# The experts' leftover rows: five blocks of 128 rows replaced by two groups of four blocks of 32 rows

## The chip, the cores and the metric

The kernel runs on one core of one Trainium2 chip. The time is that of the device in microseconds (us). A core has TensorE (PE, matrix products; its weight loads are listed as PEld), VectorE (DVE), ScalarE (ACT), GpSimd (POOL) and SyncE (SP), which run their own instruction streams in order and wait for one another through semaphores, and 16 DMA engines which all queues share.

## The reference

Two layers over x of 2 x 2048 tokens with 256 features, all in float32. Layer 0 adds gated linear attention and a product with quantised weights. Layer 1 adds softmax attention with 16 heads and, for every token, two of eight experts:

```python
logits = xf @ gate_W.T
pi = _sinkhorn(-logits)
_, top_idx = jax.lax.top_k(pi, TOP_K)
g = jnp.einsum('nd,efd->enf', xf, W_gate)
u = jnp.einsum('nd,efd->enf', xf, W_up)
y = jnp.einsum('enf,edf->end', jax.nn.silu(g) * u, W_down)
for k in range(TOP_K):
    out = out + y[top_idx[:, k], n_ar] * pi[:, k:k + 1]
```

D is 256 and F is 1024. As each of 4096 tokens goes to two experts, there are 8192 rows of expert work. With the reference's own inputs the eight experts get 1047, 977, 950, 1003, 1054, 1044, 1029 and 1088 rows.

## The kernel before

Layer 0 runs over strips of 512 tokens and leaves the sum x + layer 0 in `acc`, 128 partitions by 32 tiles of 128 tokens by 256 features (32 KB in each partition). Layer 1's attention adds to `acc` in 2 x 512-token pieces through the "chores" of `normalise`, and as soon as a 512-token piece is complete, SP writes it from `acc` to the output in memory (L1816). After that the piece of `acc` isn't used again. Attention is written as units: `scores` (L1824, tiles of 32 rows by 128 columns), the exponential on ScalarE (L1830) and `weighted_sums` (L1846), in which TensorE works in four column tiles of 128 rows by 32 columns: each tile has its own 32 stationary columns and its own moving operand, and writes its own 32 partitions of PSUM. A weighted sum comes two units after its scores.

Beside attention, VectorE runs the `router` in small steps, one for each unit: Sinkhorn, the two best experts of each token, and then `Routing.steps`, which gives each (token, expert) pair a row in a table in memory. An expert with `count` rows gets `(count + 127) >> 8` full blocks of 256 rows, and what is left over, up to 128 rows, goes to one half block of 128 rows. Room in the table that no pair takes points to a spare row of the output. `sends` fetches normed rows and scatters them into the table from POOL (L2139), each scatter behind the one before. `over` sets the flag `more` when there are more than 32 full or more than 5 half blocks; only then a branch after the usual way works through the rest.

Then come the experts: `Experts.pieces` goes through the blocks, 32 full ones with a half one after 8, 14, 20, 26 and 32 of them. For block n:

- POOL gathers its expert's weights, gate and up together 2 MB, down 1 MB (L2169), two blocks ahead; SP loads its rows (`xb`, L2185).
- `open_rows`: TensorE transposes the rows (L2207), ScalarE copies them (L2211), VectorE picks each row's routing weight and destination.
- `hidden`: for each of 8 chunks of 128 hidden features, four matmuls (L2229) with the weights stationary and the rows moving (256 columns, or 128 in a half block), then SiLU on ScalarE (L2234) and the product with up on VectorE (L2235).
- `add_rows`, one block later: 8 matmuls for each 128 rows (L2245), VectorE scales (L2250), and POOL adds the rows to the output by an indirect DMA with addition (L2254). These DMAs all write the output, so each is issued after the one before has landed.

On TensorE the order is: hidden of n, transposes of n+1, second product of n-1, hidden of n+1. A scheduler orders the instructions of each engine from the program and its data; instructions given to `keep_in_program_order` keep theirs. `rooms` hands out storage: gate and up weights go to attention's operands `operands.heads`, down weights partly there and partly to the tiles of `pt`, and all h_ps, x_ps and attention's PSUM tiles share seven banks.

Of the kernel before, what the change touches and what calls it, by code (L numbers as in the profile page):

```python
# [86 lines left out]
NHALF = NE  # L88
NBLK = NFULL + NHALF
ROWS = NFULL * BS + NHALF * BS // 2  # L90
FULLS, HALVES = 2 * B * N // BS, 5
# [132 lines left out]
def two_layers(ctx: ExitStack, tc: tile.TileContext, a: dict, out: bass.AP):  # L224
# [20 lines left out]
    )  # L245
    c.mine = const.tile([P, NBLK, NE], F32, tag="mine", name="mine")
    c.wrow = const.tile([P, NBLK], I32, tag="wrow", name="wrow")
    c.half_bias = const.tile([P, E], F32, tag="half_bias", name="half_bias")
# [10 lines left out]
    blocks = list(range(FULLS))  # L259
    for i in range(HALVES):  # L260
        blocks.insert(FULLS - 6 * i, NFULL + i)
    usual_way(tc, a, out, c, blocks)
# [4 lines left out]
    with where(c.special):  # L267
        with where(c.more):
            layer1_experts(tc, a, out, c, [b for b in range(NBLK) if b not in blocks])
        with where(c.general):  # L270
            general_way(tc, a, out, c)
# [3 lines left out]
def usual_way(ctx, tc, a, out, c, blocks):  # L275
# [27 lines left out]
    attention(tc, a, out, acc, la, norms, spans, c, operands, ready, routing, blocks, vector)  # L303
# [3 lines left out]
def general_way(ctx, tc, a, out, c):  # L307
# [17 lines left out]
    layer1_experts(tc, a, out, c, range(NBLK))  # L325
# [1359 lines left out]
def attention(  # L1685
    ctx, tc, a, out, acc, la, norms, spans, c, operands, ready, routing, blocks, vector
# [194 lines left out]
    def rooms(name, n, shape, dt=F32):  # L1881

        if name == "wgateup":
            return operands.heads[(0, 1, 3)[n % 3]].rearrange("p j t -> p (j t)")
# [25 lines left out]
    experts = Experts(tc, a, out, c, rooms, blocks)  # L1910
# [37 lines left out]
class Routing:  # L1948
# [28 lines left out]
    def steps(self, pool, psum, pi):  # L1977
# [76 lines left out]
        full, half = blocks[:, 0, :], blocks[:, 1, :]  # L2054
# [3 lines left out]
        vector.tensor_tensor(half, count, in_full, ALU.is_gt)  # L2058
        yield
        end = blocks  # L2060
        for step in (1, 2, 4):
# [12 lines left out]
        vector.tensor_tensor(away, end[:, 1, :], half, ALU.subtract)  # L2074
        vector.scalar_tensor_tensor(away, end[:, 0, :], -2.0, away, ALU.mult, ALU.add)
        vector.tensor_scalar(
            away, away, float(BS // 2), float(NFULL * BS), ALU.mult, ALU.add
# [23 lines left out]
        for n, bs in enumerate((slice(0, NFULL), slice(NFULL, NBLK))):  # L2101
# [10 lines left out]
            self.c.mine, self.eidx.unsqueeze(1).to_broadcast([P, NBLK, NE]),  # L2112
            expert.unsqueeze(2).to_broadcast([P, NBLK, NE]), ALU.is_equal,
        )
        row = tile_("row", [P, NBLK])
        vector.tensor_scalar(row, expert, float(P), self.pidx, ALU.mult, ALU.add)
        vector.tensor_copy(self.c.wrow, row)
        over = self.over
        for n, done in enumerate((FULLS, HALVES)):
# [36 lines left out]
class Block:  # L2156


    def __init__(self, e, n, b):
        self.e, self.n, self.b = e, n, b  # L2160
        self.tiles = NC if b < NFULL else NC // 2
        self.rows = self.tiles * P
        self.first = b * BS if b < NFULL else NFULL * BS + (b - NFULL) * BS // 2
# [95 lines left out]

class Experts:  # L2260


    def __init__(self, tc, a, out, c, rooms, blocks):
        self.tc, self.nc, self.a, self.out, self.c = tc, tc.nc, a, out, c
        self.rooms = rooms
        self.todo = [Block(self, n, b) for n, b in enumerate(blocks)]

    def pieces(self, begun=False):
# [4 lines left out]
        todo = self.todo  # L2273
        if not begun:
# [3 lines left out]
        for n, block in enumerate(todo):  # L2278
# [9 lines left out]
            if n and not last:  # L2288
                todo[n - 1].add_rows()
            yield  # L2290
        todo[-1].add_rows()


@with_exitstack
def layer1_experts(ctx, tc, a, out, c, blocks):
    p2 = ctx.enter_context(tc.tile_pool(name="moe", bufs=2))
    psum = ctx.enter_context(tc.tile_pool(name="moeps", bufs=2, space=PSUM))
    bufs = {"wgateup": 3, "wdown": 4, "xb": 4, "y": 4, "by": 4, "wt": 4, "to": 4,
            "h_ps": 4}

    def rooms(name, n, shape, dt=F32):
        pool = psum if name.endswith("_ps") else p2
        return pool.tile(shape, dt, tag=name, name=name, bufs=bufs.get(name, 2))

    for _ in Experts(tc, a, out, c, rooms, blocks).pieces():
        pass
# [165 lines left out]
```

## Time and profile before

| | us |
|---|---|
| median of 3 runs | 1641.2 (1638.37 to 1641.56) |
| the profiled execution | 1644.31 |
| its span, first to last instruction | 1642.5 |
| mean granted TensorE clock | 0.988 of full speed |
| L2229, hidden, 256 columns | 2048 records, 447.8 busy |
| L2229, hidden, 128 columns | 320 records, 36.7 busy |
| L2245, second product | 1104 records, 245.0 busy |
| experts, from the first L2229 to the last L2245 | 895.99 to 1630.2 |

A float32 matmul is two records, one for each of two passes, and each has its own weight load. [...]

### The profile page before, as it was taken

How to read it: one execution, taken by the hardware profiler on the slowest of the kernel's cores; microseconds unless marked ns; L12 is line 12 of the kernel's file. 1: busy time of each engine (PE TensorE's matmuls, PEld its weight loads, DVE VectorE, ACT ScalarE, POOL GpSimd, SP SyncE). 2: the span in 40 equal slices, each digit the busy share in tenths (PEclk: the TensorE clock that was granted, in tenths of full speed). 3: DMA queues.
4: the chain of work that ended last, by engine and by line, in shares of the span. 5: the costliest groups of instructions: out<-in, count | busy, mean ns of one | idle time of the engine just before them, and what ended most of it. 6: DMA issues, size and time to landing. Idle time of an engine off the chain costs nothing.

```text
span 1642.5 us, 33089 instructions
## 1 busy us (share of the span) xinstructions
PE 1587.1 (97%) x13786; PEld 1300.2 (79%) x13786; DVE 719.9 (44%) x2224; ACT 751.5 (46%) x1469; POOL 389.7 (24%) x350
## 2 busy tenths in 40 slices
PE   7789999999999999999999999999999999999997
PEld 4557676667688887888877888888898898888886
DVE  6787676564478766344353222222222222222221
ACT  5354555553688888998987211121111111111110
POOL 4342221221200003233321122222222232222221
PEclk9899999999899999999999999999999999999998
DMA  9710112213530402611144555555565565556531
GB/s 260 195 39 28 54 54 64 71 53 73 156 49 8 78 16 79 137 62 62 61 157 162 192 178 177 180 180 177 180 198 198 164 219 197 167 168 202 177 90 19
DMA packets 82510, 204.41 MB, mean 124 GB/s; under 512 B 8624, under 2 KB 64304, under 8 KB 71728
## 3 DMA queue, kind: packets, MB, share of 16 engines
q0 software_dynamic: 24944, 138.33, 26.0%
q1 hardware_dynamic: 56304, 62.71, 14.3%
q8 instruction: 110, 1.80, 0.5%
q10 hardware_dynamic: 1104, 1.18, 0.2%
q14 instruction: 48, 0.39, 0.1%
HBM read 152.26 MB, written 49.92 MB: 123 GB/s over the span
## 4 chain that ended last, share of the span: by engine, by line
PE 89%; DVE 7%; POOL 2%; DMA 1%; issue 1%; ACT 1%; POOLq 0%; SPq 0%; DVEq 0%; ACTq 0%
PE h_ps L2229 29%; PE y_ps L2245 14%; PE sc L1824 12%; PE o_ps L1846 10%; PE vf_ps L540 3%; PE y_ps L540 3%; PE f_ps L1808 2%; PE tr L590 2%; PE vg_ps L540 2%; PE g_ps L540 2%; PE qk_ps L540 1%; PE q_ps L540 1%; PE o_tr L1781 1%; PE o_ds_ps L540 1%; PE x_ps L2207 1%; PE k_ps L540 1%
## 5 line engine op out<-in xcount | busy, mean ns | idle before, releaser
L2229 PE MATMUL h_ps<-va,qk 128*128 128x256 f32 (+1 forms) x2368 | 484.5, 365 | 0.0
L2229 PEld LDWEIGHTS h_ps<-va,qk 128*128 128x128 f32 x2368 | 425.6, 190 | 53.6 <-issue 0.3
L1830 ACT ACTIVATE pt<-sc,shift 128x512 f32<-128x512 f32 (+3 forms) x687 | 405.2, 702 | 55.2 <-ACT pt L1830 26.7
L2234 ACT ACTIVATE sg<-h_ps 128x256 f32<-128x256 f32 (+1 forms) x296 | 109.4, 370 | 600.2 <-PE h_ps L2229 590.8
L2235 DVE TENSOR_TENSOR larger<-sg,h_ps 128x256 f32<-128x256 f32 (+1 forms) x296 | 119.4, 404 | 358.4 <-ACT sg L2234 346.1
L1824 PE MATMUL sc<-qk 32*128 32x128 f32 (+6 forms) x3916 | 226.0, 337 | 2.0 <-PE norm_ps L540 1.1
L1824 PEld LDWEIGHTS sc<-qk 32*128 32x128 f32 x3916 | 185.9, 187 | 37.4 <-ACT pt L1830 15.6
L1846 PE MATMUL o_ps<-pt,va 128*32 128x128 f32 (+6 forms) x3916 | 189.2, 320 | 3.1 <-DVE o_sb L114 3.1
L1846 PEld LDWEIGHTS o_ps<-pt,va 128*32 128x32 f32 x3916 | 141.2, 110 | 34.3 <-issue 9.3
L2254 POOL DMA_INDIRECT out<-va,to x69 | 109.9, 1593 | 210.9 <-DMA out<-va,to 76.2
L114 DVE TENSOR_TENSOR pt<-pt,keepmask 128x128 f32<-128x128 f32 (+3 forms) x546 | 120.0, 278 | 73.7 <-ACT pt L1830 71.9
L2245 PE MATMUL y_ps<-qk,larger 128*128 128x256 f32 x560 | 124.6, 379 | 0.1
L2250 DVE SCALAR_TENSOR_TENSOR va<-y_ps,wt,half_bias 128x256 f32<-128x256 f32 x69 | 30.4, 480 | 208.2 <-PE y_ps L2245 208.2
L2245 PE MATMUL y_ps<-larger 128*128 128x256 f32 x544 | 120.4, 379 | 0.0
L2245 PEld LDWEIGHTS y_ps<-qk,larger 128*128 128x128 f32 x560 | 104.7, 190 | 13.8 <-DVE larger L2235 0.5
L2245 PEld LDWEIGHTS y_ps<-larger 128*128 128x128 f32 x544 | 102.0, 190 | 13.1
L2139 POOL DMA_INDIRECT table<-rows,place x64 | 64.7, 1011 | 182.0 <-DMA table<-rows,place 145.2
L2169 POOL DMA_INDIRECT qk<-in_wgateup,wrow x37 | 36.8, 994 | 188.9 <-PE h_ps L2229 161.0
L540 PE MATMUL vf_ps<-qk,xnT 128*128 128x512 f32 x128 | 58.0, 606 | 0.0
L114 DVE COPY o_sb<-o_ps 128x256 f32<-128x256 f32 x64 | 27.0, 423 | 47.6 <-PE o_ps L1846 44.0
L2169 POOL DMA_INDIRECT qk<-in_wdown,wrow x19 | 18.4, 970 | 120.8 <-PE y_ps L2245 83.6
L540 PEld LDWEIGHTS vf_ps<-qk,xnT 128*128 128x128 f32 x128 | 24.0, 193 | 28.8 <-issue 25.2
(252 smaller groups left out, 1708.1 us busy)
## 6 DMA issues: line engine op xcount, KB each, us to landing
xb<-table SPq DMA_DIRECT2D x32, 265.0 KB
qk<-qk SPq DMA_DIRECT2D x32, 256.0 KB
qk<-qk SPq DMA_DIRECT2D x64, 128.0 KB
table<-spare SPq DMA_DIRECT2D x3, 2120.0 KB
va<-v SPq DMA_DIRECT2D x4, 1208.0 KB
v<-v SPq DMA_DIRECT2D x8, 574.0 KB
normed<-xn SPq DMA_DIRECT2D x8, 512.0 KB
rows<-normed POOLq DMA_DIRECT2D x16, 256.0 KB
```

Source lines behind the costliest of these rows:

```text
L114: return lambda *a, **k: self.tc.keep_in_program_order(begin(*a, **k))
L540: tc.keep_in_program_order(nc.tensor.matmul(*args, **kwargs))
L1824: nc.tensor.matmul(scs[r][:, at : at + q1 - q0], lhsT=heads[rows, 1, kb * P : (kb + 1) * P], rhs=heads[rows, 0, qt * QT + q0 : qt * QT + q ...
L1830: nc.scalar.activation(pt[:, r, 0:width], scs[r][:, 0:width], AF.Exp, bias=shift)
L1846: nc.tensor.matmul(o_ps[r * HR : (r + 1) * HR, to + q0 : to + q1], lhsT=values[b, way][:, kb, h * VC : h * VC + HR], rhs=pt[:, r, at : at ...
L2139: self.nc.gpsimd.indirect_dma_start(out=self.c.table, in_=rows[:, n, :], in_offset=None, out_offset=bass.IndirectOffsetOnAxis(ap=to[:, 2 * ...
L2169: e.nc.gpsimd.indirect_dma_start(out=w, out_offset=None, in_=e.a[name], in_offset=bass.IndirectOffsetOnAxis(ap=e.c.wrow[:, self.b : self.b ...
L2229: nc.tensor.matmul(ps[:, j, rows], lhsT=self.wgu[:, j, c, f * P : (f + 1) * P], rhs=self.xT[:, c, rows], start=c == 0, stop=c == 1,)
L2234: nc.scalar.activation(sg, ps[:, 0, rows], AF.Silu)
L2235: nc.vector.tensor_tensor(self.hT[:, f, rows], sg, ps[:, 1, rows], ALU.mult)
L2245: nc.tensor.matmul(ps[:, c, :], lhsT=self.hT[:, fc, c * P : (c + 1) * P], rhs=self.wd[:, fc, :], start=fc == 0, stop=fc == NFC - 1,)
L2254: nc.gpsimd.indirect_dma_start(out=out, out_offset=bass.IndirectOffsetOnAxis(ap=self.to[:, c : c + 1], axis=0), in_=y[:, c, :], in_offset= ...
```

## The change

The half blocks go. What an expert has left over, still up to 128 rows, goes into blocks of 32 rows, as many as it needs. Four such blocks, of whatever experts, make a `Group` of 128 table rows. The usual way works through 32 full blocks and two groups (8 small blocks); the flag `more` is set when there are more.

In a group the parts are swapped: the rows are stationary (32 columns for each block, in TensorE's four column tiles) and the weights move, 512 columns at a time for gate and up and 256 for down. The hidden values come out by row, so they are transposed in eight steps before the second product. The weights of the four blocks' experts come in three parts of 4 x 1 MB (gate, up, down), one after another, in the room of `acc`, a quarter for each block; each part is fetched when the products with the one before are issued. The steps of the groups stand at ends of full blocks: for group 0 the load after block 3, the opening after 6, gate after 7, up after 11, the transposes after 12, down after 15; for group 1 the same after 16, 19, 20, 24, 25 and 28. A group's result goes out in four scatters, one for each block, in which the rows of the other three blocks go to spare rows.

Routing counts the small blocks, has 67 block entries where it had 43, and makes `nowhere` (spare rows) and `wpart` (the rows of the half-width weights) besides. The size of the table stays as it was. The branch for `more` works through full blocks and groups in two passes; its code and that of the general way are left out here.

```diff
+SB = 32
+NSMALL = 4 * NE
+NBLK = NFULL + NSMALL
+ROWS = NFULL * BS + NSMALL * SB
+FULLS, GROUPS = 2 * B * N // BS, 2
...
-    blocks = list(range(FULLS))
-    for i in range(HALVES):
-        blocks.insert(FULLS - 6 * i, NFULL + i)
-    usual_way(tc, a, out, c, blocks)
+    usual_way(tc, a, out, c)
...
+        if name == "group_w":
+            return acc.rearrange("p t e -> p (t e)").rearrange("p (r f) -> p r f", r=4)
+        if name in ("group_b", "group_x", "group_h", "group_y"):
+            tag = {"group_b": "on", "group_x": "on", "group_h": "o_sb", "group_y": "onT"}[name]
+            return p2.tile(
+                [P, ST], F32, tag=tag, name=name, bufs=1 if tag == "onT" else 2
+            )[:, 0 : shape[1]]
+        if name == "group_s":
+            return p2.tile(shape, F32, tag="sk_equal", name=name, bufs=1)
...
-        vector.tensor_tensor(half, count, in_full, ALU.is_gt)
+        vector.tensor_tensor(small, count, in_full, ALU.is_gt)
+        for n in range(1, BS // 2 // SB):
+            one = tile_(f"small{n}", [P, NE])
+            vector.scalar_tensor_tensor(one, in_full, float(n * SB), count, ALU.add, ALU.is_lt)
+            vector.tensor_tensor(small, small, one, ALU.add)
...
+        for r in range(4):
+            rows = slice(r * SB, (r + 1) * SB)
+            vector.tensor_tensor(
+                self.c.mine[rows, NFULL:, :],
+                self.eidx[rows, :].unsqueeze(1).to_broadcast([SB, groups, NE]),
+                by_group[rows, :, r : r + 1].to_broadcast([SB, groups, NE]), ALU.is_equal,
+            )
+        yield
...
+        nowhere = tile_("nowhere_f", [P, 4])
+        vector.tensor_scalar(
+            nowhere, self.pidx.to_broadcast([P, 4]), float(SPARE), None, ALU.add
+        )
+        vector.tensor_copy(self.c.nowhere, nowhere)
+
+        for n in range(2):
+            part = tile_(f"part{n}", [P, NSMALL])
+            vector.tensor_scalar(
+                part, row[:, NFULL:], 2.0, float(n), ALU.mult, ALU.add
+            )
+            vector.tensor_copy(self.c.wpart[:, n, :], part)
...
+class Group:
+    def __init__(self, e, g):
+        self.e, self.g = e, g
+        self.b = NFULL + 4 * g
+        self.first = NFULL * BS + g * P
+        self.tiles = [slice(r * SB, (r + 1) * SB) for r in range(4)]
+
+    def gather(self, name, part):
+        e = self.e
+        rows, first = (e.c.wpart[:, part, :], NFULL) if name == "wgateup" else (e.c.wrow, 0)
+        self.w = e.rooms("group_w", 0, [P, 4, 2 * FF])
+        for r in range(4):
+            e.nc.gpsimd.indirect_dma_start(
+                out=self.w[:, r, :], out_offset=None,
+                in_=e.a[name].rearrange("r (j f) -> (r j) f", f=2 * FF),
+                in_offset=bass.IndirectOffsetOnAxis(
+                    ap=rows[:, self.b + r - first : self.b + r - first + 1], axis=0
+                ),
+            )
+
+    def load(self):
+        self.xb = self.e.rooms("group_b", 0, [P, RW])
+        load = self.e.nc.sync.dma_start(
+            out=self.xb, in_=self.e.c.table[self.first : self.first + P, :]
+        )
+        self.e.tc.keep_in_program_order(load)
+        self.gather("wgateup", 0)
...
+    def products(self, part):
+        for half in range(2):
+            ps = self.e.rooms("h_ps", half, [P, 2 * BS])
+            for c in range(2):
+                for r, rows in enumerate(self.tiles):
+                    at = c * FF + half * ST
+                    self.e.nc.tensor.matmul(
+                        ps[rows, :], lhsT=self.xT[:, c * P + r * SB : c * P + (r + 1) * SB],
+                        rhs=self.w[:, r, at : at + ST], start=c == 0, stop=c == 1,
+                    )
+            yield slice(half * ST, (half + 1) * ST), ps
+
+    def gate(self):
+        self.h = self.e.rooms("group_s", 0, [P, FF])
+        for part, ps in self.products(0):
+            self.e.nc.scalar.activation(self.h[:, part], ps, AF.Silu)
+        self.gather("wgateup", 1)
+
+    def up(self):
+        for part, ps in self.products(1):
+            self.e.nc.vector.tensor_tensor(self.h[:, part], self.h[:, part], ps, ALU.mult)
+        self.gather("wdown", 0)
...
+    def down(self):
+        nc = self.e.nc
+        ps = self.e.rooms("h_ps", 0, [P, 2 * BS])[:, 0:E]
+        for fc in range(NFC):
+            for r, rows in enumerate(self.tiles):
+                at = fc % 4 * P + r * SB
+                nc.tensor.matmul(
+                    ps[rows, :], lhsT=self.hT[fc // 4][:, at : at + SB],
+                    rhs=self.w[:, r, fc * E : (fc + 1) * E], start=fc == 0, stop=fc == NFC - 1,
+                )
+        y = self.e.rooms("group_y", 0, [P, E])
+        nc.vector.scalar_tensor_tensor(
+            y, ps, self.wt, self.e.c.half_bias, ALU.mult, ALU.add
+        )
+        for r in range(4):
+            nc.gpsimd.indirect_dma_start(
+                out=self.e.out, out_offset=bass.IndirectOffsetOnAxis(ap=self.to[:, r : r + 1], axis=0),
+                in_=y, in_offset=None, compute_op=ALU.add,
+            )
+
+    def steps(self):
+        return ((0, self.load), (3, self.open_rows), (1, self.gate), (4, self.up), (1, self.turn),
+                (3, self.down))
...
+            while between and between[0][0] <= n and not last:
+                between.popleft()[1]()
             yield
```

## The prediction

> **What bounds the kernel now.** First the page: span, engine totals, the chain that ended last.
>
> ```profile
> span 1642.5 us, 33089 instructions
> PE 1587.1 (97%) x13786; PEld 1300.2 (79%) x13786; DVE 719.9 (44%) x2224; ACT 751.5 (46%) x1469; POOL 389.7 (24%) x350
> ...
> PE 89%; DVE 7%; POOL 2%; DMA 1%; issue 1%; ACT 1%; POOLq 0%; SPq 0%; DVEq 0%; ACTq 0%
> PE h_ps L2229 29%; PE y_ps L2245 14%; PE sc L1824 12%; PE o_ps L1846 10%; PE vf_ps L540 3%; PE y_ps L540 3%; PE f_ps L1808 2%; PE tr L590 2%; PE vg_ps L540 2%; PE g_ps L540 2%; PE qk_ps L540 1%; PE q_ps L540 1%; PE o_tr L1781 1%; PE o_ds_ps
> ```
>
> 43% of the chain is the experts' two products, so a change in the experts is worth what it takes off TensorE, if nothing else gets in the way. I then read TensorE's timeline around one half block (start, length, what):
>
> ```profile
> 1040.51 13.98 PE L2229 MATMUL h_ps<-va,qk 128*128 128x256 f32 x64
> 1054.33 0.38 PE L2207 MATMUL x_ps<-ident,xb 128*128 128x128 f32 x2
> 1054.55 7.07 PE L2245 MATMUL y_ps<-larger 128*128 128x256 f32 x32
> 1061.45 7.31 PE L2229 MATMUL h_ps<-va,qk 128*128 128x128 f32 x64
> 1068.60 0.60 PE L2207 MATMUL x_ps<-ident,xb 128*128 128x128 f32 x4
> ...
> 1090.19 3.62 PE L2245 MATMUL y_ps<-qk,larger 128*128 128x256 f32 x16
> 1093.65 13.98 PE L2229 MATMUL h_ps<-va,qk 128*128 128x256 f32 x64
> ```
>
> No group has an idle gap before it: each starts when the one before has stopped issuing. So differences of starts are costs. The table of stretches agrees: TensorE 644 of 644 us busy between 950 and 1600, clock 1.00, DMA share 0.46 to 0.64 at 146 to 200 GB/s. Here only TensorE's work counts.
>
> **Part 1, the five half blocks go.** Hidden product 1061.45 to 1068.60 = 7.15; opening 1054.33 to 1054.55 = 0.22; second product 1090.19 to 1093.65 = 3.46. Sum 10.83, times 5 = 54.2 us off the path. Their 3 MB of weights each (15 MB) go too.
>
> **Part 2, two groups come.** The trace has no such group, but attention's weighted sums (L1846) run in the same tile form, 128 rows by 32 columns, four streams with different moving data:
>
> ```profile
> 878.45 1.27 PE L1824 MATMUL sc<-qk 32*128 32x128 f32 x24
> 879.64 1.07 PE L1846 MATMUL o_ps<-pt,va 128*32 128x128 f32 x24
> 880.65 1.13 PE L1808 MATMUL f_ps<-cwf,onT 128*128 128x256 f32 x4
> ```
>
> One such run streams 512 columns through each of four tiles, two passes each (an f32 matmul is two records). A full block's 64 records of 256 columns start within 13.81 us (1040.51 to 1054.33), 0.216 each, so 512 columns twice in one tile cost 4 x 0.216 = 0.863. The run takes 1.01 (879.64 to 880.65) where four tiles in turn would take 3.45: 3.4 tiles at once, or full overlap plus 0.14 for getting in and out.
>
> A group has three such sections. Gate: 2 halves x 2 contraction chunks x 4 tiles, 512 columns each, thus 4 rounds of 0.863 = 3.45. Up: the same. Down: 8 chunks x 4 tiles at 256 columns, 8 rounds of 0.432 = 3.45. Each section is entered and left once, +0.14: 3 x 3.6 = 10.8. Ten transposes of the x_ps kind (0.11 each by 0.22 for two) add 1.1, and a little for their own entry: 12.2 a group, 24.4 for two. Bounds: fully overlapped without entry cost 11.5; if the 0.14 belongs to each round of 512 columns and not to the run, 3 x 4.03 + 1.1 = 13.2. The records inside a run are 215 to 222 ns apart within a tile at 256 columns, that is full speed, so I take the entry reading.
>
> [...]
>
> The added work of other engines lies beside TensorE: per group two SiLUs and two copies of 512 columns on ACT (about 0.7 each by L1830's 702 ns) and three DVE products, on engines that are under a quarter busy there (17 to 23 of 104 us). The products are in different blocks from the steps they feed (gate at block 7, up at 11, transposes at 12, down at 15; then 20, 24, 25, 28), so each result has a block of 21.2 us to be ready. Uncovered, each would cost its own 1 to 2 us, about 8 in all.
>
> **Part 3, weights.** A group loads 3 parts of 4 MB into acc; the sum is 24 MB for 15, 9 MB over some 700 us: +13 GB/s on about 180. Each later part has four blocks (85 us) to land. The trace moved 4 MB of gathers between 845 and 860, at 280 to 423 GB/s, so a part needs 10 to 15. No wait here; if the cover were gone, a late part costs at most that, for four later parts 60 at the very worst.
>
> The first part of group 0 is issued early, in attention: the first acc quarter's gather (tiles 8 to 15) falls between table scatters at about 736, the second (tiles 0 to 7) at about 810, after batch 0's last output left acc (685.2). Each puts 1.3 us of issue and 1 MB (some 3 us) ahead of the next scatter, so the scatters end 8 to 10 us later than here:
>
> ```profile
> 843.00 0.99 POOL L2139 DMA_INDIRECT table<-rows,place  x1 [3.37 <-DMA table<-rows,place]
> 844.29 1.00 POOL L2169 DMA_INDIRECT qk<-in_wgateup,wrow  x1 [0.30 <-issue]
> 845.60 0.95 POOL L2169 DMA_INDIRECT qk<-in_wgateup,wrow  x1 [0.30 <-issue]
> 882.51 1.02 POOL L2169 DMA_INDIRECT qk<-in_wdown,wrow  x1 [35.96 <-PE sc L1824]
> ```
>
> Behind them wait the first two blocks' weights and, on SP, their rows (845.67). They have landed by about 861, where the bytes moved fall from 327 to 72 GB/s; rows are used at 887.3, weights at 896.0. Ten us later leaves 16 and 25 us: cost nothing; beyond that each us costs one. The other two quarters stand in POOL's order after the first weights of the second product (883.8) and wait for acc's last outputs, issued by SP at 882.5 and 907.9. Queued behind them: block 2's weights (893.6 now, used at 934.7) and block 3's (914.3, used at 955.9). A few us late, still 20 early.
>
> On POOL a group's four scatters each wait for the one before: 4 x 4.6 us alone, 6 to 8 under gathers. At block 15 they alternate with group 1's first gathers, and block 19's weights come some 15 us later than now. They are issued two blocks plus a second product ahead (49 us), so 30 remain. Nothing.
>
> Routing gets some 16 small DVE operations (0.16 each, 2.6 us) and one more step; DVE is 11.7 to 18.8 of 30 us busy there. I charge 0.5, range 0 to 3: they delay masks which have two units in hand. By the reference's inputs the experts' counts exceed 4 x 256 by 23, 30, 20, 5 and 64 in five experts: 6 pieces of 32, and two groups hold 8, so the extra branch isn't taken.
>
> **Part 4, the end.** The last block is now a full one.
>
> ```profile
> 1626.60 3.62 PE L2245 MATMUL y_ps<-qk,larger 128*128 128x256 f32 x16
> ...
> 1627.22 1.56 POOL L2254 DMA_INDIRECT out<-va,to  x1 [3.02 <-DVE larger L2235]
> 1630.26 0.48 DVE L2250 SCALAR_TENSOR_TENSOR va<-y_ps,wt,half_bias 128x256 f32<-128x256 f32 x1 [2.86 <-PE y_ps L2245]
> 1632.62 1.56 POOL L2254 DMA_INDIRECT out<-va,to  x1 [3.84 <-DMA out<-va,to]
> ```
>
> Now the single last scatter starts 2.5 us after TensorE stops (1630.1), held by block 31's second one. After, two scatters follow the last product: the first about 1.0 after TensorE (1612.55 to 1613.51 at the block before), the second 4.6 later, at 5.6. That is +3.1 us.
>
> **The sum.** -54.2 + 24.4 + 3.1 + 0.5 = -26.2. The profiled execution took 1644.3 (span 1642.5 and 1.8 around it), 3.1 above the runs' median of 1641.2. Against its own time: 1618.1, span about 1616. Against the median: **1615.0**.
>
> **Rivals.**
> - A, full overlap, everything else hidden: as above; with the bounds 11.5 to 14.6 a group 1613 to 1620, with DVE's 3 us up to 1623. For it: L1846's runs. Chance 0.75.
> - B, two of four tiles at a time, since matmuls here stream 512 columns where L1846's reach 256 at most: section 6.9, group 21.9, -54.2 + 43.8 + 3.6 = -6.8: 1634. Against: at 256 columns the tiles overlap whichever pieces come first. Chance 0.06.
> - C, POOL or the weights come late somewhere (the alternation at block 15, the start of the experts): A plus 5 to 15, 1620 to 1630, at 1625. For it: POOL's queue is in order and its scatters wait; against: 30 and 16 us of slack. Chance 0.13.
> - D, the tiles run in turn: section 13.8, group 42.5, two 85; -54.2 + 85 + 3.6 = +34: 1676, slower. It decides as soon as fewer than 1.7 of four tiles overlap (a group over 25.3 us). Against: 3.4 by the row. Chance 0.04.
> - E, the end's +3.1 is hidden or other small gains: 1611. Chance 0.02.
> - That the change doesn't take the work off TensorE isn't possible short of D.
>
> **Numbers.** Measuring this kernel tells about 0.2% (3.3 us) from no change. Faster: A, C, E and most of B: 0.95; same 0.01; slower, D and a C far beyond its price: 0.04. B and D (0.10) and the ends of A and C are left out of the range, and a few us added below for E: 1609 to 1629. The likeliest case alone is 1613 to 1620.
>
> **What would show it.** In the profile after: h_ps with 128x128 gone; groups of 32 records of 128*32 with 512 columns in 3.5 to 3.7 us each, twice gate and up, and 64 with 256 columns in the same; full blocks still 21.16 apart without idle TensorE; the last scatter about 5.6 us after TensorE's end; table scatters ending near 852. Wrong if such a section takes 4.5 or more (B, D), or TensorE waits for acc, wgateup or wdown (C).

## The result and the profile after

The changed kernel takes 1615.8 us, the median of 4 runs (1614.35 to 1618.65); the kernel before took 1639.8 beside it (1636.19 to 1641.56). The ratio is 0.9858, 95% interval 0.9835 to 0.9882, so it is faster by about 24 us. The prediction was 1615.0 in 1609 to 1629, a change of -26.2 from 1641.2. In two later sets the changed kernel took 1622.5 (ratio 0.9883, 0.9864 to 0.9902) and 1620.8 (0.9867, 0.9844 to 0.9889), and the kernel before 1641.9 and 1643.7, so the measured change is -24.0, -19.3 and -22.9. That the first set missed the forecast by only 0.8 us is partly luck, since the kernel before came out 1.4 faster there than the forecast's base. What follows is read from distances inside a trace.

The page of the changed kernel, as of before: span, engine totals, the chain that ended last.

```profile
span 1612.5 us, 32728 instructions
...
PE 1554.2 (96%) x13652; PEld 1254.7 (78%) x13652; DVE 712.3 (44%) x2200; ACT 742.2 (46%) x1434; POOL 406.4 (25%) x367
...
PE 88%; DVE 7%; POOL 2%; ACT 1%; DMA 1%; issue 1%; SPq 0%; POOLq 0%; DVEq 0%; ACTq 0%
```

TensorE is busy 1554.2 us where it was 1587.1, and the chain is still TensorE's. Its timeline around the three sections of group 0 (start, length, what):

```profile
1035.63 0.38 PE L2333 MATMUL h_ps<-ident,group_b 128*128 128x128 f32 x2
1035.85 13.98 PE L2267 MATMUL h_ps<-va,qk 128*128 128x256 f32 x64
1049.67 0.60 PE L2245 MATMUL x_ps<-ident,xb 128*128 128x128 f32 x4
1050.10 7.07 PE L2283 MATMUL y_ps<-larger 128*128 128x256 f32 x32
1057.11 3.64 PE L2356 MATMUL h_ps<-acc,group_x 128*32 128x512 f32 x32
1060.68 14.08 PE L2267 MATMUL h_ps<-va,qk 128*128 128x256 f32 x64
1074.59 0.60 PE L2245 MATMUL x_ps<-ident,xb 128*128 128x128 f32 x4
1075.03 7.07 PE L2283 MATMUL y_ps<-larger 128*128 128x256 f32 x32
1081.94 13.98 PE L2267 MATMUL h_ps<-va,qk 128*128 128x256 f32 x64
...
1170.35 1.04 PE L2379 MATMUL h_ps<-ident,group_s 128*128 128x128 f32 x8
1171.22 13.98 PE L2267 MATMUL h_ps<-va,qk 128*128 128x256 f32 x64
...
1234.79 3.66 PE L2391 MATMUL h_ps<-acc,group_h 128*32 128x256 f32 x64
1238.38 14.08 PE L2267 MATMUL h_ps<-va,qk 128*128 128x256 f32 x64
```

From start to start the gate section costs 3.57 us (1057.11 to 1060.68) and the down section 3.59 (1234.79 to 1238.38); the up section at 1145.51 costs 3.57 too. (Between traces the down section varies more: it takes 3.66 and 3.68 in a second trace of the same kernel.) No row has an idle gap before it. Rows overlap, because a record is shown longer than the distance to the next one of its tile (592 and 429 ns in the gate section), so lengths do not add up and distances of starts do. Entering and leaving the tile form also costs a little in the neighbours: the second product before the section is 7.01 long from start to start where an ordinary one is 6.91 (1075.03 to 1081.94), the hidden product after it 13.91 where one behind a full-width product takes 13.82.

The table of stretches (TensorE's busy us first; then granted clock, DMA share, GB/s at the end of each row):

```profile
1000.00:1100.00 100.00, 100.00 (x490) 85.57 (x489) 21.69 (x67) 18.69 (x45) 26.94 (x22) 1.00 0.61 198
1100.00:1300.00 200.00, 200.00 (x1011) 172.25 (x1010) 43.13 (x120) 33.99 (x83) 60.38 (x48) 1.00 0.67 214
1300.00:1500.00 200.00, 200.00 (x980) 171.19 (x979) 43.54 (x126) 35.53 (x86) 53.94 (x44) 1.00 0.64 210
```

TensorE is full in all of it at full clock, while the DMA engines move 198 to 214 GB/s, the added weights included. The end, where two scatters now follow the last product:

```profile
1589.02 7.07 PE L2283 MATMUL y_ps<-larger 128*128 128x256 f32 x32
...
1596.12 0.88 DVE L2288 SCALAR_TENSOR_TENSOR va<-y_ps,wt,half_bias 128x256 f32<-128x256 f32 x2 [6.07 <-PE y_ps L2283]
1596.88 1.56 POOL L2292 DMA_INDIRECT out<-va,to  x1 [10.90 <-DVE va L2288]
1601.38 1.55 POOL L2292 DMA_INDIRECT out<-va,to  x1 [2.94 <-DMA out<-va,to]
```

For the experiments three distances are read in every trace: "experts", from the first weight load of the first hidden product to TensorE's end (the start of its last weight load and 0.22 us); "last scatter", from that end to the start of the last scatter; and "rest", from there to the end of the span.

| kernel | first hidden product at | experts | last scatter | rest | first hidden product to end of span |
|---|---|---|---|---|---|
| before | 895.98 | 733.86 | 2.78 | 9.89 | 746.53 |
| after | 891.10 | 704.61 | 5.67 | 11.12 | 721.40 |
| difference | | -29.25 | +2.89 | +1.23 | -25.13 |

### The profile page after: what moved, and what is told of

Its sections match the earlier page's. It is cut to its first block, busy times and chain, and to the rows that moved or that the text cites. A ratio compares the mean times of both kernels' runs of the same rounds, so it can differ in the third digit from the quotient of the medians.

```text
span 1612.5 us, 32728 instructions
## 1 busy us (share of the span) xinstructions
PE 1554.2 (96%) x13652; PEld 1254.7 (78%) x13652; DVE 712.3 (44%) x2200; ACT 742.2 (46%) x1434; POOL 406.4 (25%) x367
## 4 chain that ended last, share of the span: by engine, by line
PE 88%; DVE 7%; POOL 2%; ACT 1%; DMA 1%; issue 1%; SPq 0%; POOLq 0%; DVEq 0%; ACTq 0%
PE h_ps L2267 28%; PE y_ps L2283 14%; PE sc L1826 12%; PE o_ps L1848 10%; PE vf_ps L542 3%; PE y_ps L542 3%; PE f_ps L1810 2%; PE tr L592 2%; PE vg_ps L542 2%; PE g_ps L542 2%; PE qk_ps L542 1%; PE q_ps L542 1%; PE o_ds_ps L542 1%; PE o_tr L1783 1%; PE h_ps L2356 1%; PE x_ps L2245 1%
## 5 line engine op out<-in xcount | busy, mean ns | idle before, releaser
L2267 PE MATMUL h_ps<-va,qk 128*128 128x256 f32 x2048 | 448.6, 379 | 0.0
L2267 PEld LDWEIGHTS h_ps<-va,qk 128*128 128x128 f32 x2048 | 388.1, 190 | 57.0 <-issue 4.5
L2272 ACT ACTIVATE sg<-h_ps 128x256 f32<-128x256 f32 x256 | 98.2, 384 | 529.9 <-PE h_ps L2267 529.9
L2273 DVE TENSOR_TENSOR larger<-sg,h_ps 128x256 f32<-128x256 f32 x256 | 107.9, 422 | 344.1 <-ACT sg L2272 344.1
L2292 POOL DMA_INDIRECT out<-va,to x64 | 101.8, 1591 | 178.6 <-DMA out<-va,to 56.5
L2283 PE MATMUL y_ps<-qk,larger 128*128 128x256 f32 x512 | 113.8, 379 | 0.1
L2283 PE MATMUL y_ps<-larger 128*128 128x256 f32 x512 | 113.2, 379 | 0.0
L2283 PEld LDWEIGHTS y_ps<-larger 128*128 128x128 f32 x512 | 96.2, 190 | 12.5
L2283 PEld LDWEIGHTS y_ps<-qk,larger 128*128 128x128 f32 x512 | 95.8, 190 | 12.7 <-DVE larger L2273 0.5
L2207 POOL DMA_INDIRECT qk<-in_wgateup,wrow x32 | 31.5, 984 | 143.7 <-PE h_ps L2267 137.0
L542 PEld LDWEIGHTS vf_ps<-qk,xnT 128*128 128x128 f32 x128 | 24.2, 194 | 29.0 <-issue 25.6
```

Source lines behind the costliest of these rows:

```text
L542: tc.keep_in_program_order(nc.tensor.matmul(*args, **kwargs))
L2207: e.nc.gpsimd.indirect_dma_start(out=w, out_offset=None, in_=e.a[name], in_offset=bass.IndirectOffsetOnAxis(ap=e.c.wrow[:, self.b : self.b ...
L2267: nc.tensor.matmul(ps[:, j, rows], lhsT=self.wgu[:, j, c, f * P : (f + 1) * P], rhs=self.xT[:, c, rows], start=c == 0, stop=c == 1,)
L2272: nc.scalar.activation(sg, ps[:, 0, rows], AF.Silu)
L2273: nc.vector.tensor_tensor(self.hT[:, f, rows], sg, ps[:, 1, rows], ALU.mult)
L2283: nc.tensor.matmul(ps[:, c, :], lhsT=self.hT[:, fc, c * P : (c + 1) * P], rhs=self.wd[:, fc, :], start=fc == 0, stop=fc == NFC - 1,)
```

## The experiments

**The kernel before, again.** Does the start of the experts, 4.9 us earlier in the trace after, belong to the change?

> The kernel before, unchanged, for a second profile of it. In the first pair of profiles the experts begin 4.9 us earlier after the change (891.1 for 896.0), though nothing before them was meant to be faster. Theory (play between executions): this profile's experts begin somewhere between 889 and 897, and the medians of the two kernels differ by 24 to 28. Rival (the change's other order of routing's steps makes attention 4 to 5 us faster): 896 again within 1 us, and all profiles of changed kernels near 891.

Measured: 1642.1 us (1637.6 to 1646.9, 20 runs), ratio 0.9999 (0.999 to 1.0009). The first hidden product starts at 892.35, the experts take 733.86 as before, the last scatter starts 2.47 after TensorE. So that start moves by some us from one execution of one kernel to the next. Over all the traces it lies between 891.1 and 897.9 whatever the kernel; the 4.9 us are no gain of the change.

One part of the way there does differ between the kernels: the end of routing. The four rows are the kernel before (L1752, L1808) and the changed one (L1754, L1810). `within` is the last flag that VectorE works out for the router, and TensorE sums it.

```profile
622.44 0.19 PE L1752 MATMUL d_ps<-ones_mat,within 128*1 128x1 f32 x2 [0.67 <-DVE within L114]
...
633.02 1.13 PE L1808 MATMUL f_ps<-cwf,onT 128*128 128x256 f32 x4
```

```profile
625.64 0.19 PE L1754 MATMUL d_ps<-ones_mat,within 128*1 128x1 f32 x2 [1.82 <-DVE within L117]
...
632.51 1.13 PE L1810 MATMUL f_ps<-cwf,onT 128*128 128x256 f32 x4
```

From the last placing product of routing (`place_ps`, at 584.16 before and 582.28 after) to this f_ps product it is 48.86 us before and 50.23 after. Over the traces it is 48.83 and 48.86 for the kernel before, and 49.76 to 51.64 in all twelve of changed kernels: 0.9 to 2.8 us more. No group has loaded weights by then, and the kernel without groups has 50.50, so what is left as the cause is the change in routing. TensorE waits 1.62 to 1.82 us for `within`, where it was 0.67. Behind that wait its granted clock (third number from the end) falls, which it does in neither trace of the kernel before; first the row of before, then of after:

```profile
625.00:630.00 5.00, 3.63 (x74) 2.96 (x78) 4.69 (x26) 3.32 (x7) 2.63 (x3) 1.00 0.08 29
```

```profile
625.00:630.00 5.00, 4.14 (x54) 3.40 (x55) 4.69 (x25) 2.36 (x4) 2.30 (x5) 0.66 0.17 57
```

In the trace's clock records it is half the full clock for 3.4 us in seven of the twelve traces (49.76 to 50.55 us from product to product) and for 6.8 us in the other five (51.58 to 51.64). Whether the longer wait brings the half clock on was not shown: no run changes it alone.

Behind this stretch the way to the experts takes 258.6 to 263.4 us, 262.97 and 261.86 for the kernel before. That is play, as variation from one execution to the next is called here: the trace of before has 3.4 us of half clock of its own at 847.6 there, which its repetition has not.

**Without the groups.** What do they cost, and what are the half blocks worth? The rows left over are then in no block; the expectation says so.

```diff
-    experts = Experts(tc, a, out, c, rooms, range(FULLS), range(GROUPS))
+    experts = Experts(tc, a, out, c, rooms, range(FULLS), ())
```

> The two groups are left out whole: their loads, products and scatters (142 rows of expert work are missing in the output); the half blocks stay out too. Theory (a group costs what it takes on TensorE, all else lies beside it): minus 2 x 12.0 = 24 us against the changed kernel, 1592; against the kernel before minus 48 = 54.2 for the half blocks less the longer end and some of the start's play. Rival (the groups' 24 MB of weights, POOL's extra scatters or the two early gathers in attention delay something): more than 24, so 1580 to 1588.

Measured: 1592.2 us (1589.25 to 1593.33), ratio 0.9695 (0.9673 to 0.9717), as expected. The experts take 679.77. Against the kernel before, this stage lacks only the half blocks, so the five of them were worth 733.86 - 679.77 = 54.09, and the two groups cost 704.61 - 679.77 = 24.84, 12.42 each. The pieces in the timeline after give the same: three sections of 3.57 to 3.59 and 0.19 beside, 0.87 for the eight transposes, 0.22 for two, make 12.4.

**Without five of the six weight parts.** Are the groups' weights hidden? Of the 24 MB only the first part, 4 MB, is loaded, and the groups compute with it throughout.

```diff
         e = self.e
+        if e.todo and (self.g or part or name == "wdown"):
+            return
```

> Of the groups' six weight parts only the first (4 MB) is loaded; the five later ones (20 MB, 20 gathers on POOL) are left out and all products take what lies there, so the small blocks' results are not the reference's. TensorE's work is the same. Theory (the weights are hidden): 1616, within 2 us of the changed kernel. Rival (late weights or DMA contention cost part of the gain): 3 to 10 us faster, 1606 to 1613.

Measured: 1619.2 us (1617.47 to 1624.88), ratio 0.9871 (0.9851 to 0.9892). The experts take 704.92 where they take 704.61 to 704.77 with all weights (three traces). Nothing is won by leaving 20 MB out: they are hidden. The first 4 MB are left out only together with the groups, and there too the experts start no earlier than elsewhere (896.18).

**Less cover.** How much of the four blocks between a part's load and its use is needed? Up then stands one block behind its load, down two.

```diff
-        return ((0, self.load), (3, self.open_rows), (1, self.gate), (4, self.up), (1, self.turn),
-                (3, self.down))
+        return ((0, self.load), (3, self.open_rows), (1, self.gate), (1, self.up), (1, self.turn),
+                (1, self.down))
```

> The groups' steps stand closer: up one block after gate (it was four), down one block after the transposes (it was three). The second weight part then has about 21 us from its first gather to its use, the third about 42. Theory (a part of 4 MB needs 10 to 15 us to land, and its last three gathers are issued 9 us after the first): up is fed just in time, waits of 0 to 3 us in each group, 1616 to 1622. Rival (one block is ample: DMA has enough to spare): 1616, no wait. Rival (with a block's own 3 MB beside it a part needs over 25 us): 4 to 8 us of wait for each group, 1624 to 1632.

Measured: 1619.3 us (1617.58 to 1621.83), ratio 0.9862 (0.9839 to 0.9886); experts 705.04. POOL's and TensorE's timelines from the gate section to the up section of group 0, one block apart:

```profile
1062.32 3.64 PE L2356 MATMUL h_ps<-acc,group_x 128*32 128x512 f32 x32
...
1087.25 3.64 PE L2356 MATMUL h_ps<-acc,group_x 128*32 128x512 f32 x32
1090.82 14.08 PE L2267 MATMUL h_ps<-va,qk 128*128 128x256 f32 x64
```

```profile
1066.22 0.98 POOL L2313 DMA_INDIRECT acc<-in_wgateup,wpart  x1 [0.67 <-PE h_ps L2356]
...
1074.44 0.94 POOL L2313 DMA_INDIRECT acc<-in_wgateup,wpart  x1 [0.30 <-issue]
```

The four quarters of up's weights are issued between 1066.22 and 1074.44, the last three behind an output scatter that waits; the up section starts at 1087.25, still right behind the second product and 3.57 long. So a part had landed within 21 us of its first issue. In the changed kernel a quarter (1 MB) lands 5.7 to 9.7 us after its issue, and for up three of the four blocks of cover are spare. Down kept two blocks, some 43 us (1091.15 to 1134.21); less was not tried.

**The tiles in turn.** Does TensorE need the order in which neighbouring instructions go to different tiles? This run puts all of one tile's matmuls ahead of the next tile's: in gate and up that makes runs of 4 records (2 contraction chunks, two records each) on one tile, in down runs of 16.

```diff
-            for c in range(2):
-                for r, rows in enumerate(self.tiles):
+            for r, rows in enumerate(self.tiles):
+                for c in range(2):
...
-        for fc in range(NFC):
-            for r, rows in enumerate(self.tiles):
+        for r, rows in enumerate(self.tiles):
+            for fc in range(NFC):
```

> The same group work, with the loops over the four blocks and the contraction chunks exchanged, so that all of one column tile's matmuls stand together in the order. Theory (four tiles at once is what makes a group cheap, and TensorE takes its matmuls in order): a section of gate, up or down grows from 3.57 to about 13.7 us, 6 sections, +61 us on the changed kernel: 1677, slower than the kernel before by 37. Rival (TensorE finds the free tile whatever the order, or the gain is from the rows left out and not from the overlap): 1616, sections stay near 3.6.

Measured: 1635.7 us (1633.55 to 1636.99), ratio 0.9959 (0.9945 to 0.9972). That is not the 61 us expected but some 16; the experts take 720.44, 15.8 more than after. Its timeline:

```profile
1063.92 3.68 PE L2356 MATMUL h_ps<-acc,group_x 128*32 128x512 f32 x32
1067.52 14.08 PE L2267 MATMUL h_ps<-va,qk 128*128 128x256 f32 x64
...
1241.67 11.50 PE L2391 MATMUL h_ps<-acc,group_h 128*32 128x256 f32 x64
1253.11 14.08 PE L2267 MATMUL h_ps<-va,qk 128*128 128x256 f32 x64
```

The gate section still takes 3.60: in runs of 4 the tiles overlap in full although their matmuls no longer alternate in the program. The down section takes 11.44 where in turn it would take 13.8. The starts of its records show why: 12 records of the first tile start alone, 216 ns apart; from the 13th on each has one of the second tile beside it, for 4 records; then the second tile goes on alone for 8, and so on. (A record does not name its tile. This reading goes by the starts, and by the tile's first record being shown 403 ns long and the others 379.) So by the starts of this trace, the next tile's records begin when four of the tile before are left to start. An estimate from that is 3 x 12 + 16 = 52 record times of 0.216 us, 11.23, and with 0.14 for entry, from L1846's run, 11.4.

**Runs of eight.** That reading makes a forecast for a length not tried: with 8 records in a run, only the last four of each tile overlap with the next tile's first four.

```diff
-        for half in range(2):
-            ps = self.e.rooms("h_ps", half, [P, 2 * BS])
-            for c in range(2):
-                for r, rows in enumerate(self.tiles):
+        both = [self.e.rooms("h_ps", half, [P, 2 * BS]) for half in range(2)]
+        for r, rows in enumerate(self.tiles):
+            for half, ps in enumerate(both):
+                for c in range(2):
...
-        for fc in range(NFC):
+        for fh in range(2):
             for r, rows in enumerate(self.tiles):
+                for fc in range(4 * fh, 4 * fh + 4):
```

> The tiles in turn again, in runs of 8 records on one tile: gate and up go through both halves and both chunks of one block before the next (512 columns), down through 4 chunks of one block before the next (256 columns). With runs of 4 records nothing was lost before, with runs of 16 a section took 11.4. Theory (up to 4 records of one tile can be out at once, and a fifth holds everything behind it): a run of 8 lets the next tile start after 4 records; gate and up take 20 x 0.43 + 0.14 = 8.8 us each, down 36 x 0.216 + 0.14 = 7.9; together +14.8 a group, +29 in all, 1645. Rival 1 (the window holds 8 records or more and the 11.4 has another reason): about 3.6 each, 1616. Rival 2 (strict order as soon as a run is over 4): 13.8 each, 1677.

Measured: 1649.3 us (1646.83 to 1651.65), ratio 1.0047 (1.0027 to 1.0066): slower than the kernel before.

```profile
1062.16 8.86 PE L2356 MATMUL h_ps<-acc,group_x 128*32 128x512 f32 x32
1070.95 14.08 PE L2267 MATMUL h_ps<-va,qk 128*128 128x256 f32 x64
...
1250.29 8.17 PE L2393 MATMUL h_ps<-acc,group_h 128*32 128x256 f32 x64
1258.39 14.08 PE L2267 MATMUL h_ps<-va,qk 128*128 128x256 f32 x64
```

Gate and up take 8.79 each, down 8.10. For gate and up the forecast is 3 x 4 + 8 = 20 times of 0.429, 8.58, and 0.14 for entry makes 8.72; for down it is 36 times of 0.216, 7.78, and 0.14 makes 7.92. Measured are 8.79 and 8.10, so 0.07 and 0.18 are left over. The records start as it says: 0, 454, 883, 1312 ns alone, then in pairs from 1741 and 1748 on, and the last four alone. The experts take 734.50, 29.7 over the changed kernel's 704.76 in its set, and 2 x (2 x 5.22 + 4.51) = 29.9 is what the sections are longer. So the gain depends on the order of the matmuls within a section: by this one choice the change would have been a loss.

**The last rows early.** The last block's product for its second 128 rows goes to a PSUM tile of its own, so the first 128 rows needn't wait for it.

```diff
+        ps = [ps[:, c, :] for c in range(self.tiles)]
+        if last:
+            ps[1] = self.e.rooms("h_ps", 0, [P, 2 * BS])[:, 0:E]
...
-            todo[-1].add_rows()
+            todo[-1].add_rows(True)
```

> The changed kernel, but the last block's second product writes its second 128 rows to another PSUM bank, so that its first 128 rows can be scaled and scattered while TensorE still works on the second. Theory (after the last product two scatters in a row set the end, 5.7 us after TensorE stops): the first scatter starts some 2.5 us before TensorE's end, the last one 2.1 to 2.3 after it, so 3.4 us less, 1612 to 1613, about 0.2% below the changed kernel in the same set. Rival (what follows the last scatter, POOL's own closing, decides and starts no earlier): no change.

Measured: 1615.9 us (1614.93 to 1618.48), ratio 0.9842 (0.9822 to 0.9862). Beside it the changed kernel again:

> The changed kernel unchanged, for a second profile and for pairs in the same set: 1616 within 2, ratio to the kernel before 0.984 to 0.988; experts' stage (first hidden product to the last second product) 704.6 to 705.0 in this profile too, while its start may lie anywhere between 889 and 898.

It took 1622.5 us (1617.76 to 1624.1), ratio 0.9883 (0.9864 to 0.9902). In the edited kernel the last scatter starts 2.35 after TensorE's end, in the changed one 5.69. The end of the edited kernel's timeline:

```profile
1595.10 3.62 PE L2286 MATMUL y_ps<-larger 128*128 128x256 f32 x16
...
1598.55 3.62 PE L2286 MATMUL h_ps<-larger 128*128 128x256 f32 x16
1598.76 0.48 DVE L2291 SCALAR_TENSOR_TENSOR va<-y_ps,wt,half_bias 128x256 f32<-128x256 f32 x1 [2.62 <-PE y_ps L2286]
1599.52 1.56 POOL L2295 DMA_INDIRECT out<-va,to  x1 [7.51 <-DVE va L2291]
1602.21 0.48 DVE L2291 SCALAR_TENSOR_TENSOR va<-h_ps,wt,half_bias 128x256 f32<-128x256 f32 x1 [2.97 <-PE h_ps L2286]
1604.14 1.55 POOL L2295 DMA_INDIRECT out<-va,to  x1 [3.07 <-DMA out<-va,to]
```

The first scatter now starts at 1599.52, while TensorE still works, and the second follows 4.62 later. The medians differ by 6.6 us, the traces (first hidden product to end) by 721.42 - 718.52 = 2.9. To see which holds, both ran again:

> The changed kernel with the last block's two halves of output rows in tiles of their own, once more, now beside the changed kernel in as many rounds. By the first look's trace the last scatter starts 2.3 us after TensorE's end where it was 5.7, and the span from the first hidden product to the end is 718.5 for 721.4. So the time is 3 to 3.4 us under the changed kernel's in this set; if the 6.6 us between the two medians of the first set were real, there would be a second effect of 3 us that the trace does not show.

> The changed kernel again, beside the two runs above: 1616 to 1622 us by its two sets so far.

Measured: 1619.4 us (1617.31 to 1620.58), ratio 0.9857 (0.984 to 0.9873), and 1620.8 (1617.58 to 1626.2), ratio 0.9867 (0.9844 to 0.9889). The traces give 718.46 and 721.65, again 3.2 apart; the medians 1.4. So the edit is worth about 3 us by the traces, and the rest of the 6.6 did not come again; the timed runs alone do not settle a gain this small. By the traces it is the version to take.

**POOL's closing.** Of the end's +4.1 us, 2.9 are the scatters and 1.2 lie behind them. In the trace's records the last long thing in the span is POOL closing: an instruction INC_SWDGE_SEM and a DRAIN, 1.08 and 3.66 us before, 1.38 and 4.89 after. In the traces so far both grew with the number of transfers that POOL had issued. This run adds 32 transfers of 64 bytes that nothing reads:

```diff
         self.wd = self.gather("wdown").rearrange("p (c d) -> p c d", c=NFC)
+        few = self.e.rooms("few", self.n, [P, 16])[0:1, :]
+        self.e.nc.gpsimd.dma_start(out=few, in_=self.e.a["wdown"][0:1, 0:16])
```

> The changed kernel with one small transfer more for each of the 32 blocks, issued by POOL beside the block's second weights: 64 bytes into a tile that nothing reads, 32 transfers of 64 bytes in all. In the runs so far POOL's closing at the very end grew with the number of transfers that POOL had issued: with 208, 220, 223 and 240 of them its DRAIN took 2.438, 3.377, 3.663 and 4.888 us and its INC_SWDGE_SEM 0.780, 1.010, 1.080 and 1.380. If the number is the cause: with 272 the DRAIN takes 4.89 + 32 x 0.077 = 7.3 us, INC_SWDGE_SEM 1.38 + 32 x 0.019 = 2.0, the end of TensorE to the end of the span 16.8 + 3.1 = 19.8, and the time is 3.1 us over the changed kernel's in this set. If the closing follows the bytes that were gathered, or the state of the queue at the end, it stays at 4.9 and 1.4, and the time with it. The experts' stage itself stays at 704.6 to 705.0 either way.

Measured: 1618.3 us (1616.04 to 1620.14), ratio 0.9851 (0.9835 to 0.9868), not slower than the changed kernel. The closing became shorter. The theory falls; a second one, a count that starts again at each multiple of 64, was tried with 20 small transfers on top of the early last rows (the same edit, under `if self.b < 20`):

> The changed kernel with two edits: the last block's two halves of output rows in tiles of their own, and 20 small transfers of 64 bytes issued by POOL beside the second weights of the first 20 blocks, 260 transfers by POOL in all. The run with 32 such transfers overturned the theory that the closing grows with their number: at 272 the DRAIN took 2.438 us and INC_SWDGE_SEM 0.772, as at 208, with 4.888 and 1.380 at 240 between them. New theory: the closing goes by the number since the last multiple of 64 (16, 28, 31, 48 and again 16 gave 2.438, 3.377, 3.663, 4.888 and 2.438). Then 260 is 4 beyond 256: DRAIN 2.44 - 12 x 0.077 = 1.5, INC_SWDGE_SEM 0.77 - 12 x 0.019 = 0.55, together 4.2 under the changed kernel's 6.27. The last scatter 2.3 after TensorE's end, so TensorE's end to the span's end is 16.8 - 3.4 - 4.2 = 9.2 us. The time against the kernel before in its set is 0.9815 to 0.984, for 0.9858 to 0.9883 of the changed kernel in its three sets. If instead the small transfers themselves shorten the closing whatever their number, the DRAIN stays between 2.4 and 4.9; if the kind of the early transfers matters, it is 2.44.

Measured: 1614.5 us (1611.07 to 1615.04), ratio 0.9837 (0.9821 to 0.9853); DRAIN 5.09 us. The second theory falls too:

| transfers by POOL | kernel | INC_SWDGE_SEM, us | DRAIN, us |
|---|---|---|---|
| 208 | without groups | 0.780 | 2.438 |
| 220 | first part only | 1.010 | 3.377 |
| 223 | before, twice | 1.080 | 3.663 |
| 240 | after (three times), tiles in turn, runs of eight, last rows early (twice) | 1.380 | 4.888 |
| 240 | one block of cover | 1.360 | 4.807 |
| 260 | last rows early, 20 small ones more | 1.425 | 5.092 |
| 272 | 32 small ones more | 0.772 | 2.438 |

The number alone doesn't set it, and neither does its remainder by 64: two kernels with 240 transfers differ, and 272 transfers have half the DRAIN of 260. What does is open. This last kernel's time is the early last rows' own: from the first hidden product its trace is 718.63 long, for 718.52 and 718.46 without the 20 transfers.

## Why the prediction was right

**Part 1, -54.2.** Measured -54.1. Starts of neighbouring groups on a TensorE without gaps gave the cost within 0.1.

**Part 2, +24.4.** Measured +24.8. The section forecast, 3.6 us from attention's weighted sums, came out at 3.57 to 3.59. Going by L1846's row was right: 13.81 us for four tiles one after another against 3.57 is 3.9 tiles at once. No run shows the 14.6 a group of rival A's bounds, nor the 4.5 a section of the prediction's last line; the runs showed 12.42 and 3.57 to 3.59. Of the two readings of L1846 (3.4 tiles at once, or full overlap and a fixed entry) it was the entry: within the gate section four records start within 20 ns, the next four 453 ns after the first, and each four after those 429 to 430 ns later. What the sum left out is that the form also lengthens its neighbours, by 0.19 a section, 1.1 us in all.

The premise of rival D about order, though, was too strict. Tiles in turn at 13.8 a section takes program order for the order of work. The runs of 4, 8 and 16 records show 3.60, 8.79 (8.10 in down) and 11.44: by the starts in the traces with 8 and 16, the next tile's first four records stand beside this one's last four. A rival of that kind is real, 1649 us with runs of eight, but it needs long runs on one tile, which this change doesn't have.

**Part 3, 0.** Right in the sum: the experts take 704.92 without five of six parts against 704.61, and 705.04 with one block of cover before up. Two sizes in it were wrong, both on the safe side. The table scatters were to end 8 to 10 us later, near 852; POOL's timeline after has

```profile
801.99 0.97 POOL L2179 DMA_INDIRECT table<-rows,place  x1 [2.27 <-DMA table<-rows,place]
...
804.29 1.00 POOL L2313 DMA_INDIRECT acc<-in_wgateup,wpart  x1 [0.16 <-DVE pt L117]
805.60 1.00 POOL L2179 DMA_INDIRECT table<-rows,place  x1 [0.30 <-issue]
811.30 0.98 POOL L2179 DMA_INDIRECT table<-rows,place  x1 [4.70 <-DMA table<-rows,place]
...
841.88 0.96 POOL L2179 DMA_INDIRECT table<-rows,place  x1 [2.83 <-DMA table<-rows,place]
```

The gather's issue fits in front of a scatter that would have been waiting, and only the scatter behind it lands late: 5.70 between the scatters, where 2.7 to 4.4 is usual around it. From first to last, the scatters take 226.0 to 228.6 us in the three traces without the gathers and 224.6 to 233.2 in the eleven with them (medians 228.0 and 230.5): some 2.5 us for two gathers, not 8 to 10. And block 19's weights at the alternation were to be 15 us late:

```profile
1256.81 1.59 POOL L2402 DMA_INDIRECT out<-group_y,group_to  x1 [1.92 <-DMA out<-group_y,group_to]
1258.70 0.98 POOL L2207 DMA_INDIRECT qk<-in_wgateup,wrow  x1 [0.30 <-issue]
```

They could have been issued at 1252.3, when block 16's hidden product had ended, and are 6.4 late: the four-way alternation runs at 4 to 6 us a step, not 6 to 8. Either way TensorE did not wait.

**Routing, +0.5, range 0 to 3.** Too small, though inside its range: 0.9 to 2.8 us. Two steps failed. The prediction's 11.7 to 18.8 of 30 us are VectorE's load between 690 and 750 us. Routing's last steps run before 630, where VectorE is busy 4.69 of 5 us in the row of the kernel before, so the added operations move what follows them. And they were to delay only masks; what they delayed is `within`, for which TensorE waits. The half clock behind that wait was in no term.

**Part 4, +3.1.** The scatters' part is +2.9 against the profiled run of before, +3.2 against its repetition. What the part had wrong is where the end lies: it stopped at the last scatter's start and held the rest of the span as fixed. The rest grew by 1.23 us between the two first traces (9.89 and 10.22 in two of before; 11.12, 10.97 and 11.08 in three of after), and POOL's DRAIN and INC_SWDGE_SEM in it by 1.53 together.

**The sum.** From the first hidden product to the end: -54.09 + 24.84 + 2.89 + 1.23 = -25.13, where the same terms were predicted as -54.2 + 24.4 + 3.1 = -26.7. This difference repeats: from first hidden product to end the two traces of before have 746.53 and 746.55, the three of after 721.40, 721.42 and 721.65. With routing's 0.9 to 2.8 it makes -24.2 to -22.3, and the three sets' medians differ by -24.0, -19.3 and -22.9. The 3 us that the second set lacks are open; play of that size ahead of the experts is seen. The profiled execution came at 1614.35, below the forecast's 1618.1, because its experts began 4.9 us earlier, most of which is such play. So the result is near the forecast because the two large terms were right; the smaller ones were 0.4, 1.0 and 0.4 to 2.3 too low, and the number in the first set hides that by luck.

## What to carry to other kernels

In column tiles that hold different weights, put neighbouring instructions on different tiles; runs of four records on one tile cost 0.03 us a section here (3.60 for 3.57), runs of eight more than doubled it (8.79 for 3.57, 8.10 for 3.59). Where a stage keeps TensorE full, cost an added section from start to start and look at its neighbours as well, and price the end to the last instruction of the span, not to the last transfer's start. Read an engine's load in the very stretch where its work is added. Before crediting a few us to a change, run the kernel before a second time and compare the distance inside the trace that the change touches.

## What the hardware showed that was not expected

Between column tiles the records of these sections did not start strictly in program order. With 4, 8 and 16 records in a run on one tile, the sections took 3.60, 8.79 or 8.10, and 11.44 us, where one tile after another was estimated at 13.8. In the trace with 16, a record of the next tile starts beside each of a tile's last four, from the 13th on; in the trace with 8, pairs start from 1741 and 1748 ns on. This is read from the starts, as a record does not name its tile.

TensorE's wait for VectorE in mid-attention was 1.62 to 1.82 us in the twelve traces of changed kernels and stood in all of them right before 3.4 or 6.8 us of half clock (a mean of 0.66 from 625 to 630 us in the first trace after). In the two traces of the kernel before, where the wait was short (0.67 in the first), the clock there stayed at 1.00. That the one causes the other was not shown.

The closing of POOL at the end of these kernels varied between 3.2 and 6.5 us (INC_SWDGE_SEM and DRAIN together) with small changes in what POOL had issued before, not in the number's order; its cause is open.
